# Three graph attention layers: the list of sources from five gathers of long pieces, and big and small blocks of nodes by turns

## The chip, the cores and the metric

The kernel runs on one core of a Trainium2 chip. The metric is the device time of one execution in microseconds, and the median of the runs is what counts. The engines are called as in the profile: PE is TensorE, DVE is VectorE, ACT is ScalarE, POOL is GpSimd and SP is SyncE. POOL issues all indirect DMAs (gathers), SP most of the plain ones.

## The reference

There are N = 6,250 nodes with 256 features each, and E = 100,000 edges given as `src` and `dst`, sorted by `dst`. A node has 16 incoming edges on average. Two layers with 4 heads of 64 features come first, with a self-loop added to each node, and an elu between them; then a residual and a layer norm; then a layer with 8 heads of 32 features, a residual and a layer norm:

```python
def _gatv2_layer(x, src, dst, n, Wl, Wr, att, b):          # layers 1 and 2
    xl = (x @ Wl).reshape(n, H, C)
    xr = (x @ Wr).reshape(n, H, C)
    e = jax.nn.leaky_relu(xl[src] + xr[dst], NEG_SLOPE)
    logits = jnp.einsum('ehc,hc->eh', e, att)
    # softmax of the logits over the edges of each dst -> alpha
    msg = xl[src] * alpha[:, :, None]
    return segment_sum(msg, dst).reshape(n, H * C) + b

def third_layer(h, W, a, src, dst):                         # layer 3
    Wh = jnp.einsum('nf,hfd->hnd', h, W)
    e = jax.nn.leaky_relu(s1[:, src] + s2[:, dst], ALPHA)   # s1 = Wh.a1, s2 = Wh.a2
    # softmax over the edges of each dst -> attn
    return segment_sum(attn[:, :, None] * Wh[:, src], dst)

x = _layernorm(x + layer2(elu(layer1(x))))
x = _layernorm(x + third_layer(x))
```

All is float32. The indices are known only on the chip.

## The kernel before, in words

**Columns and blocks.** The nodes are sorted by their number of incoming edges and cut into 49 blocks of 128, one node to a partition. `columns` works out from E and N alone how many sources per node a block may have to hold: 27 for the first block (its few longer lists are treated apart, with one extra gathered row), then 25, 24, 23, 22, 21, 21, and so on down to 9 in the last. The sum is 803. A block of c columns needs c gathers: each brings one row of the layer's table (1 KB and a little more) for each of 128 nodes.

**The plan** (`make_plan`). It finds each node's sources and its place in the sorted order. The steps that matter here run in this order on DVE: `count` (incoming edges of each node, from products on PE), `begin_i` (L993, where a node's list begins), then the sort: `oh`, `cum` (scans), `place_f`, `to`, then three wide products `to_hi`, `given`, `to_lo` (L1080), which PE multiplies into `pp` (L1085): the node that stands at each sorted place. Then come `lacking` and `fill` for six spans of nine blocks (L1013: entries beyond a node's count are set to "no node"), `node_i` from `pp`, and `fits`, a check on which the main path rests. Beside this POOL gathers the lists: 49 times (L998) a piece of CM = 38 sources for each of 128 nodes, where the program's own numbering puts node b*128 + p on partition p. `fill` writes each span to `near_d` in HBM.

```python
    for k in range(NB):                                    # L998
        nc.gpsimd.indirect_dma_start(out=near[:, k, :], in_=listed, in_offset=begin_i[:, k])
```

(The call is shortened.) `tables(n)` puts the next n of the 49 blocks of the first table x @ Wl through PE (transposes and a product), ACT (copies) and SP (writes to `xl_d`). The order of every engine is the order of the program text; no scheduler reorders it. 27 tables stand ahead of the sort's last products, 22 behind `pp`. Spans 0 and 1 of `fill` stand before `node_i`, span 2 after the `fits` products, span 3 seven tables later, spans 4 and 5 behind the last table.

**The layers** (`tile_by_degree`). Each of layers 1 and 2 goes through the 49 blocks in order. POOL gathers one block ahead of the one in work, as far as a ring of 9 row tiles (`rows`, 9 columns to a tile) has room:

```python
            for b in range(NB):
                if b + 3 < NB: start(b + 3)
                if b + 1 < NB: gather(b + 1)               # POOL, L1235
                if b + 2 == NB: follow()                   # early gathers of the next layer
                if b + 1 < NB: ready(b + 1)                # the next block's own products
                rows, cut, wt, new = attend(b)             # DVE: z, lg; ACT: exps
                if b: rest = end(b - 1, acc, den)
                den = new(); nc.vector.reciprocal(den, den)
                acc = weighted_sum(...)                    # DVE: g * wt; PE: acc, L1418
```

For each row tile `attend` makes three passes on DVE (L1504 to L1506): a maximum that does the leaky ReLU, a product with `att`, and a sum to the logits `lg`. ACT makes the exps into `wt`. `weighted_sum` multiplies rows by weights on DVE (L1411) and ACT (L1410), and PE adds the columns up into `acc` with one product of the identity per column. The last steps of block b-1 (its row of the next layer's table, over PE, ACT and SP) run beside this. A gather of a layer reads any row of that layer's table, so it has to wait until all 49 blocks have been written by the layer before.

`EARLY = (14, 12, 11)` softens that: in layer 1, `sort_sources` sorts the lists of blocks 0, 1 and 2 by number, and the first 14, 12 and 11 columns of these, which lie in all blocks but the last four (`LATE`), are gathered at the end of the layer before (the index tile is `soon`). That is 37 early gathers for layer 2 and 37 for layer 3.

Layer 3 has no z passes, its logits come with the gathered row. DVE multiplies rows by weights (L1433) and adds columns up (L1442). POOL puts each finished block out, one put to a block.

Of the kernel before, what the change touches and what calls it, by code (L numbers as in the profile page):

```python
# [26 lines left out]
F32 = mybir.dt.float32  # L27
BF16 = mybir.dt.bfloat16
I32 = mybir.dt.int32
# [6 lines left out]
P = 128  # L36
# [4 lines left out]
RUNS = 64  # L41
EARLY = (14, 12, 11)
LATE = 4


def columns(E, N, NB):

    mean = E / N
    pmf = [math.exp(-mean)]
    for k in range(1, 200):
        pmf.append(pmf[-1] * mean / k)
    over, sd = [], []
    for c in range(199):
        p = sum(pmf[c + 1 :])
        g = sum((k - mean) * pmf[k] for k in range(c + 1, 200))
        over.append(N * p)  # L60
        sd.append(math.sqrt(max(N * (p * (1.0 - p) - g * g / mean), 0.0)))
    cols = []
    for b in range(NB):
        most = P * b
        cols.append(next(
            c for c in range(199) if (over[c] + 3.5 * sd[c] <= most if b else over[c] < 0.01)
        ))
    low = max((c for c in range(199) if N - over[c] <= P // 4), default=0)
    high = next(c for c in range(199) if over[c] <= P // 4)
    pmf += [0.0] * 200  # L70
    held = next(
        c for c in range(199)
        if N * sum((k - c) * pmf[k] for k in range(c, 200))
        + 3.5 * math.sqrt(N * sum((k - c) ** 2 * pmf[k] for k in range(c, 200))) <= P
    )
    assert cols[1] <= held < cols[0]
    return cols, low, high, held

# [636 lines left out]
def make_plan(  # L715
# [20 lines left out]
    assert (NP + 1) << SHIFT < 1 << 24 and NB % PART == 0  # L736

    one = ctx.enter_context(tc.tile_pool(name="plan_one", bufs=1))
    tmp = ctx.enter_context(tc.tile_pool(name="weights", bufs=2))
# [5 lines left out]
    dram = ctx.enter_context(tc.tile_pool(name="list_dram", bufs=1, space=DRAM))  # L745
    list_d = dram.tile([-(-E // CM) * CM + CM], I32, name="list_d")

# [123 lines left out]
    if rest:  # L871
# [8 lines left out]
    diff = iota("diff_f", [P, P], [[1, P]], mult=-1)  # L880
    nothing = filled_tile("nothing", [1, list_d.shape[0] - E], 0, I32)
    nc.gpsimd.memset(next_e, NP)
    left(0, nc.gpsimd)
    a = next(d for d in range(512, 0, -16) if E % d == 0)
    nc.scalar.dma_start(list_d[E:].unsqueeze(0), nothing)
    nc.scalar.dma_start(
        list_d[:E].rearrange("(a b) -> a b", a=a), src.rearrange("(a b) -> a b", a=a)
    )
    each = iota("each", [P, P, T], [[1, P], [0, T]], dtype=BF16)
    x_end = filled_tile("x_end", [P, F], 0.0)  # L890
    far = filled_tile("far", [P, CM], NP, I32)
    ranks = iota("ranks", [P, CM], [[1, CM]])
    ones = filled_tile("ones_f", [P, P], 1.0)
    ones_b = filled_tile("ones_b", [P, P], 1.0, BF16)
# [47 lines left out]
    for what in "lar":  # L942
# [3 lines left out]
    part = one.tile([P, 3, RUNS], I32, name="part")  # L946
    nc.vector.tensor_scalar(
        part[:, 0, :], run_i, SHIFT, P - 1, op0=OP.logical_shift_right, op1=OP.bitwise_and
    )
    nc.vector.tensor_single_scalar(part[:, 1, :], run_i, SHIFT + 7, op=OP.logical_shift_right)  # L950
    nc.vector.tensor_single_scalar(part[:, 2, :], run_i, (1 << SHIFT) - 1, op=OP.bitwise_and)
# [25 lines left out]


    pc = ps.tile([P, 2, NB], F32, name="pc", tag="ph")
    nc.tensor.matmul(pc[:, 0, :], ones, count, start=True, stop=True)  # L980
    nc.tensor.matmul(pc[:, 1, :], above, count, start=True, stop=True)
    key = one.tile([P, NB], BF16, name="key_b")
    nc.vector.tensor_scalar(key, count, float(high), float(low), op0=OP.min, op1=OP.max)
    nc.vector.tensor_scalar(key, key, -1.0, float(high), op0=OP.mult, op1=OP.add)
    block = one.tile([P, NB], F32, name="block")
    nc.vector.tensor_copy(block, pc[:, 0, :])
    upto = one.tile([P, NB], F32, name="upto")
    nc.vector.tensor_tensor_scan(upto, ones_k[:, :NB], block, 0.0, op0=OP.mult, op1=OP.add)
    from_f = one.tile([P, NB], F32, name="from_f")
    nc.vector.tensor_sub(from_f, upto, block)  # L990
    nc.vector.tensor_add(from_f, from_f, pc[:, 1, :])
    begin_i = one.tile([P, NB], I32, name="begin_i")
    nc.vector.tensor_scalar(begin_i, from_f, float(E), 0.0, op0=OP.min, op1=OP.max)  # L993
    near = one.tile([P, NB, CM], I32, name="near")
    no = one.tile([P, NB, CM], I32, name="no")
    listed = list_d.rearrange("(a b) -> a b", b=CM)
    for k in range(NB):
        nc.gpsimd.indirect_dma_start(  # L998
            out=near[:, k, :], out_offset=None, in_=listed,
            in_offset=bass.IndirectOffsetOnAxis(ap=begin_i[:, k : k + 1], axis=1),  # L1000
        )
    spans = [(k, min(NB, k + 9)) for k in range(0, NB, 9)]
# [8 lines left out]
    def fill(k0, k1):  # L1011
        shape = [P, k1 - k0, CM]
        nc.vector.copy_predicated(  # L1013
            near[:, k0:k1, :], no[:, k0:k1, :], far[:, None, :].to_broadcast(shape)
        )
        nc.sync.dma_start(
            near_d[k0 * P : k1 * P, :CM].rearrange("(k p) c -> p k c", p=P).bitcast(I32),
            near[:, k0:k1, :],
        )


    tables(1)
    oh = one.tile([P, KEYS, NB], BF16, name="oh")
    nc.vector.tensor_tensor(
        oh, steps, key[:, None, :].to_broadcast([P, KEYS, NB]), op=OP.is_equal
    )
    ohf = oh.rearrange("p k b -> p (k b)")
# [22 lines left out]
    nc.vector.tensor_single_scalar(piece[:, 0, :], place, P - 1, op=OP.bitwise_and)  # L1050
    nc.vector.tensor_single_scalar(piece[:, 1, :], place, 7, op=OP.logical_shift_right)
    nc.vector.tensor_scalar(vals[:, 2, :], count, 255.0, None, op0=OP.min)
    to = one.tile([P, 2, NB], BF16, name="to")
# [3 lines left out]
    with nc.allow_non_contiguous_dma(reason="one number to a row"):  # L1057
        nc.scalar.dma_start(
            xl1_d[:NP, W2:].rearrange("(b p) w -> p b w", p=P), place_f.unsqueeze(2)
        )  # L1060
# [25 lines left out]
    for k in spans:  # L1086
        lacking(*k)
    fill(*spans[0])
    fill(*spans[1])
    got = one.tile([P, 3, NB], F32, name="got")  # L1090
    nc.vector.tensor_copy(got, pp)
    nc.vector.scalar_tensor_tensor(
        node_i, got[:, 1, :], float(P), got[:, 0, :], op0=OP.mult, op1=OP.add
    )

    wrong = one.tile([P, KE + NB + 1], F32, name="wrong")
    nc.vector.tensor_tensor(wrong[:, : KE - 1], dst_e[:, : KE - 1], dst_e[:, 1:], op=OP.is_gt)
    nc.vector.tensor_tensor(wrong[:, KE - 1 : KE], dst_e[:, KE - 1 :], next_e, op=OP.is_gt)  # L1100
    nc.vector.tensor_tensor(wrong[:, KE : KE + NB], got[:, 2, :], most, op=OP.is_gt)
    nc.vector.tensor_scalar(
        wrong[:, KE + NB :], upto[:, NB - 1 :], float(E), None, op0=OP.not_equal
    )
# [14 lines left out]
    right(1)  # L1119
    fill(*spans[2])  # L1120
    for c in range(2):
# [4 lines left out]
    tables(7)  # L1126
    fill(*spans[3])
    for k, b in enumerate(biases):
# [8 lines left out]
    tables(NB)  # L1137
    for k in spans[4:]:
        fill(*k)


@with_exitstack
def tile_by_degree(
# [52 lines left out]
    few_row = consts.tile([P, max(W2 + 1, A1)], F32, name="few_row")  # L1196
    soon = consts.tile([P, len(EARLY), max(EARLY)], I32, name="soon")
    late = consts.tile([P, len(EARLY)], F32, name="late")
# [118 lines left out]
    def begin(own, table, width):  # L1317

        for b, n in enumerate(EARLY):
            begun[b] = row_tiles(b, own)  # L1320
            gather_rows(b, *begun[b], own, table[:AHEAD], soon, width, 0, n)

    def sort_sources(work, ps, b):
# [9 lines left out]
        for r in range(0, CK, 8):  # L1333
# [5 lines left out]
        nc.vector.tensor_single_scalar(spots[:, b, :n], places[:, :n], KEY, op=OP.logical_shift_right)  # L1339
        e = EARLY[b]  # L1340
        nc.vector.tensor_single_scalar(soon[:, b, :e], spots[:, b, :e], AHEAD - 1, op=OP.min)
        nc.vector.tensor_single_scalar(
            late[:, b : b + 1], spots[:, b, e - 1 : e], float(AHEAD), op=OP.is_ge
        )
        if b + 1 == len(EARLY):
            pb = ps.tile([P, b + 1], F32, name="pb", tag="tp")
            nc.tensor.matmul(pb, ones, late, start=True, stop=True)
            bad = work.tile([P, 1], F32, name="bad")
            nc.vector.reduce_sum(bad, pb, axis=AX.X)
            nc.vector.tensor_single_scalar(done, bad, 0.0, op=OP.is_equal)  # L1350
# [115 lines left out]
    def layer2(i, table, of, width, start, own, finish, follow):  # L1466
# [5 lines left out]
        with ExitStack() as es:  # L1472
# [24 lines left out]
            def attend(b):  # L1497
# [29 lines left out]
                if i == 0:  # L1527
                    for g, (s0, s1) in zip(rows, cut):
                        s = max(s0, 1)
                        nc.scalar.copy(spots[:, b, s - 1 : s1 - 1], g[:, s - s0 : s1 - s0, W2])  # L1530
                    if 0 < b <= len(EARLY):
                        sort_sources(work, pst, b - 1)
# [260 lines left out]
```

## Time and profile before

| | before |
|---|---|
| median of 3 runs | 3365.79 us (3364.47 to 3366.1) |
| profiled execution | 3880.55 us, span 3878.7 us |
| mean granted TensorE clock in it | 0.665 |
| busy in the span | PE 1481.8, DVE 2836.2, ACT 1091.1, POOL 2530.5 us |
| first row gather of layer 1 | 154.5 us from the span's start |
| layer 1, first to last reciprocal | 201.8 to 1494.1 us |
| layer 2 | 1542.0 to 2704.1 us |
| layer 3 | 2747.5 to 3862.5 us |

The rows from the third on come from the one profiled execution, which took 515 us more than the median. The times within it are therefore for comparing parts with each other, and not shares of the 3365.79 us. A line of a group reads: source line, engine, operation, output<-input, count, then busy time in all, mean duration in ns, and the idle time of the engine just before these instructions, with what ended most of it. A line of a timeline reads: start, duration, engine, source line, operation, and in brackets the idle time before it and what ended it.

### The profile page before, as it was taken

What the parts mean: (1) busy time and instruction counts of PE and PEld (TensorE: products, weight loads), DVE (VectorE), ACT (ScalarE), POOL (GpSimd) and SP (SyncE); (2) the same over time, 40 slices, a digit from 0 to 9 for tenths busy, and PEclk for the clock granted to TensorE, in tenths of its full rate; (3) what the DMA queues carried; (4) which work ended last, traced back from release to release, by engine and by line L of the source; (5) the groups of instructions that cost most, each with busy time, mean ns of one, the idle gap of its engine ahead of it and who ended that gap; (6) DMA issues with size and microseconds to landing.
All of it is one profiled execution on the core that took longest, in us unless ns stands there. A gap on an engine that the chain in (4) does not pass through costs nothing.

```text
span 3878.7 us, 23608 instructions
## 1 busy us (share of the span) xinstructions
PE 1481.8 (38%) x5130; PEld 1113.8 (29%) x5130; DVE 2836.2 (73%) x2648; ACT 1091.1 (28%) x4176; POOL 2530.5 (65%) x2613
## 2 busy tenths in 40 slices
PE   6324665556667763355544545554000000000000
PEld 5213444434555542343433433443000000000000
DVE  6228988668888876899876988896676565666665
ACT  3113444334445442243433434443000000000000
POOL 6464666666666645666666666664777777777774
PEclk8656877778788886676666677776555555555555
DMA  8532333333434334333433434442343333333332
GB/s 188 109 92 78 98 104 104 100 99 103 105 102 108 104 79 109 100 106 104 112 107 105 111 107 110 109 111 74 101 108 101 96 97 96 97 97 96 97 97 57
DMA packets 196123, 395.60 MB, mean 102 GB/s; under 512 B 63036, under 2 KB 115514, under 8 KB 195956
## 3 DMA queue, kind: packets, MB, share of 16 engines
q0 software_dynamic: 122048, 338.04, 33.2%
q1 hardware_dynamic: 66226, 54.22, 5.1%
q10 hardware_dynamic: 7698, 1.74, 0.4%
q8 instruction: 45, 0.74, 0.1%
q14 instruction: 106, 0.87, 0.1%
HBM read 353.82 MB, written 40.42 MB: 102 GB/s over the span
## 4 chain that ended last, share of the span: by engine, by line
issue 20%; POOL 20%; DVE 13%; PE 10%; another core or an unknown queue 6%; ACT 5%; DMA 1%; DVEq 0%; POOLq 0%; ACTq 0%
POOL g L1235 18%; PE acc L1418 6%; DVE z L1505 4%; DVE z L1504 4%; DVE lg L1506 3%; PE pm L1362 3%; ACT g L1410 2%; ACT wt L1381 2%; DVE g L1411 1%; POOL out L1733 1%; DMA g<-xl_d,near_r 1%; DVE weighted L1433 1%; ACT xT L1357 0%; PE pt L1355 0%
## 5 line engine op out<-in xcount | busy, mean ns | idle before, releaser
L1235 POOL DMA_INDIRECT g<-xl_d,near_r x1569 | 1487.4, 948 | 858.7 <-issue 454.3
L1418 PE MATMUL acc<-g,ident 128*128 128x256 f32 x3408 | 1015.9, 461 | 765.3 <-issue 282.7
L1418 PEld LDWEIGHTS acc<-g,ident 128*128 128x128 f32 x3408 | 774.4, 234 | 1004.2 <-issue 522.3
L1235 POOL DMA_INDIRECT g<-whs_d,near_r x766 | 793.2, 1036 | 284.2 <-issue 250.0
L1410 ACT ACTIVATE g<-g,by 128x64 f32<-128x64 f32 x2056 | 545.1, 337 | 316.1 <-issue 310.8
L1504 DVE TENSOR_TENSOR z<-g,pr 128x1820 f32<-128x1820 f32 (+4 forms) x234 | 497.1, 2125 | 19.1 <-DMA g<-xl_d,near_r 10.0
L1505 DVE TENSOR_TENSOR z<-z,at 128x1820 f32<-128x1820 f32 (+4 forms) x234 | 497.4, 2126 | 8.0
L1506 DVE TENSOR_REDUCE lg<-z 128x28 f32<-128x1820 f32 (+4 forms) x234 | 497.3, 2125 | 8.1
L1442 DVE TENSOR_REDUCE acc_v<-weighted 128x256 f32<-128x4096 f32 (+15 forms) x49 | 343.7, 7014 | 16.5 <-remote 8.3
L1411 DVE TENSOR_TENSOR g<-g,wt 128x1792 f32<-128x1792 f32 (+8 forms) x234 | 348.4, 1505 | 2.9
L1391 ACT ACTIVATE wt<-lg 128x128 f32<-128x128 f32 (+17 forms) x49 | 14.0, 285 | 851.0 <-DVE top L1374 391.5
L1703 DVE TENSOR_TENSOR lg<-g,s_r 128x56 f32<-128x56 f32 (+4 forms) x111 | 22.1, 213 | 315.1 <-DMA g<-whs_d,near_r 272.5
L1357 ACT COPY xT<-pt 128x256 f32<-128x256 f32 x147 | 54.9, 374 | 688.5 <-remote 342.2
L1433 DVE TENSOR_TENSOR weighted<-g,wt 128x1792 f32<-128x1792 f32 (+4 forms) x111 | 226.6, 2056 | 0.1
L1571 DVE RECIPROCAL den<-den 128x4 f32<-128x4 f32 x98 | 17.4, 177 | 212.9 <-ACT wt L1381 165.2
L1381 ACT ACTIVATE wt<-lg,top 128x19 f32<-128x19 f32 (+14 forms) x392 | 116.0, 296 | 190.8 <-DVE lg L1506 74.3
L1362 PE MATMUL pm<-wcat,xT 128*128 128x260 f32 x392 | 136.0, 505 | 56.3 <-ACT xT L1357 49.8
L1362 PE MATMUL pm<-wh_cat,xT 128*128 128x272 f32 x196 | 77.5, 531 | 183.8 <-ACT xT L1357 95.5
L1537 DVE TENSOR_TENSOR h<-acc,den 128x256 f32<-128x256 f32 x98 | 40.7, 416 | 126.2 <-remote 112.8
L1362 PEld LDWEIGHTS pm<-wcat,xT 128*128 128x128 f32 x392 | 94.8, 255 | 90.5 <-ACT xT L1357 64.6
L1362 PEld LDWEIGHTS pm<-wh_cat,xT 128*128 128x128 f32 x196 | 42.8, 242 | 203.0 <-ACT xT L1357 104.7
L1362 PE MATMUL pl<-wcat,xT 128*128 128x260 f32 x196 | 64.0, 455 | 55.5 <-issue 40.4
(232 smaller groups left out, 1548.4 us busy)
## 6 DMA issues: line engine op xcount, KB each, us to landing
g<-xl_d,near_r POOLq DMA_INDIRECT x1569
g<-whs_d,near_r POOLq DMA_INDIRECT x766
whs_d<-row SPq DMA_DIRECT2D x49, 132.0 KB
xl_d<-xl SPq DMA_DIRECT2D x49, 130.0 KB
xl_d<-row SPq DMA_DIRECT2D x49, 130.0 KB
xr_d<-row SPq DMA_DIRECT2D x49, 130.0 KB
two<-xl_d SPq DMA_DIRECT2D x49, 130.0 KB
two<-xr_d SPq DMA_DIRECT2D x49, 130.0 KB
```

What stands on the lines that cost most here:

```text
L1235: nc.gpsimd.indirect_dma_start(out=g[:, j + own - s0, :width], out_offset=None, in_=table, in_offset=source(of, b, j),)
L1357: nc.scalar.copy(xT, pt)
L1362: nc.tensor.matmul(pm, xT[:, c, :], w[:, c, :], start=c == 0, stop=c == 1)
L1381: nc.scalar.activation(wt[:, :, h], lg[:, :S, h], AF.Exp, bias=top[:, h : h + 1], accum_out=den[:, h : h + 1],)
L1410: nc.scalar.mul(g4[:, t, h, :], g4[:, t, h, :], by[:, t - m, h : h + 1])
L1411: nc.vector.tensor_mul(g4[:, :m], g4[:, :m], wt[:, s0 : s0 + m, :].unsqueeze(3).to_broadcast([P, m, H, F // H]),)
L1418: nc.tensor.matmul(acc, ident, g4[:, t], start=s0 + t == 0, stop=s0 + t == S - 1 and not more)
L1433: nc.vector.tensor_mul(prod[:, s0 - base : s1 - base, :].rearrange("p t (h d) -> p t h d", h=H), g[:, :n, :F].rearrange("p t (h d) -> p t ...
L1442: nc.vector.reduce_sum(part, prod[:, : s1 - base, :].rearrange("p s f -> p f s"), axis=AX.X)
L1504: nc.vector.tensor_max(z, g[:, :n, :W2], xr[:, None, :].to_broadcast([P, n, W2]))
L1505: nc.vector.tensor_mul(z, z, at[:, None, :].to_broadcast([P, n, W2]))
L1506: nc.vector.reduce_sum(lg[:, s0:s1, :], z.rearrange("p t (h d) -> p t h d", h=H2), axis=AX.X)
```

## The change

It has three parts.

1. **Five gathers instead of 49.** The nodes are numbered p*49 + b during the plan, so that partition p holds 49 nodes in sequence and their lists lie one after the other in the sorted edge list. Five gathers (one for each ten nodes) bring pieces of LONG = 309 sources. Node k of a piece would begin at 16k (less a lead of 64) if each node had 16 edges; the real place differs by 0 to 127, `off_i`. DVE moves each list into place bit by bit: for the bit of 64, while it copies out of the piece (10 copies and 10 predicated copies), then for the bits of 32 to 1 with six predicated copies over all 50 slots. All this stands before the sort (`cum` and so on) in DVE's order; `oh` is moved ahead too.
2. **Big and small blocks by turns.** `columns` returns 27, 9, 25, 10, 24, 10, 23, 11, 22, 11, 21, 12, ... 16, 16 in place of the descending order, in all three layers and their tables. In the plan `place_f` and `piece` are changed to match (four small DVE instructions).
3. **EARLY** becomes {0: 14, 2: 12}: block 1 now has 9 columns and none early; two blocks are sorted in layer 1 instead of three.

All six fills now stand together ahead of `node_i`, and so, in SP's queue, between the 27th and the 28th table. The diff, cut to its core:

```diff
-EARLY = (14, 12, 11)
+EARLY = {0: 14, 2: 12}
@@ columns
-    return cols, low, high, held
+    turns = [0] * NB
+    for r, c in enumerate(cols):
+        turns[min(2 * r, 2 * NB - 1 - 2 * r)] = c
+    return turns, low, high, held
@@ make_plan
+    SEGS, STEP, BITS = 5, 10, 7
+    LEAD = 1 << BITS - 1
+    MEAN = E // N
+    LONG = MEAN * (STEP - 1) + CM + 2 * LEAD - 1
+    WIDE = CM + LEAD - 1
...
-    nc.tensor.matmul(pc[:, 0, :], ones, count, start=True, stop=True)
-    nc.tensor.matmul(pc[:, 1, :], above, count, start=True, stop=True)
+    total = one.tile([P, 1], F32, name="total")
+    nc.vector.reduce_sum(total, count, axis=AX.X)
+    nc.tensor.matmul(pc[:, 1:], above, total, start=True, stop=True)
+    nc.tensor.matmul(pc[:, :1], ones, total, start=True, stop=True)
...
+    for k in range(SEGS):
+        nc.gpsimd.indirect_dma_start(
+            out=piece_of[:, k, :], out_offset=None, in_=listed,
+            in_offset=bass.IndirectOffsetOnAxis(ap=begin_i[:, k : k + 1], axis=1),
+        )
...
+    nc.vector.tensor_scalar(off_i, off, 0.0, float(2 * LEAD - 1), op0=OP.max, op1=OP.min)
+    for k in range(BITS):
+        nc.vector.tensor_scalar(
+            bit[:, k], off_i, k, 1, op0=OP.logical_shift_right, op1=OP.bitwise_and
+        )
+    moved = one.tile([P, SEGS, STEP, WIDE], I32, name="moved")
+    for k in range(STEP):
+        for first_at in (0, LEAD):
+            data = piece_of[:, :, MEAN * k + first_at : MEAN * k + first_at + WIDE]
+            if first_at == 0:
+                nc.vector.tensor_copy(moved[:, :, k, :], data)
+            else:
+                nc.vector.copy_predicated(
+                    moved[:, :, k, :],
+                    bit[:, BITS - 1, :, k : k + 1].to_broadcast([P, SEGS, WIDE]), data,
+                )
+    every = moved.rearrange("p s j w -> p (s j) w")
+    bits = bit.rearrange("p b s j -> p b (s j)")
+    for k in range(BITS - 2, -1, -1):
+        n = CM + (1 << k) - 1
+        nc.vector.copy_predicated(
+            every[:, :, :n], bits[:, k, :].unsqueeze(2).to_broadcast([P, SEGS * STEP, n]),
+            every[:, :, 1 << k : (1 << k) + n],
+        )
+    near = every[:, :NB, :CM]
-    for k in range(NB):
-        nc.gpsimd.indirect_dma_start(
-            out=near[:, k, :], out_offset=None, in_=listed,
-            in_offset=bass.IndirectOffsetOnAxis(ap=begin_i[:, k : k + 1], axis=1),
-        )
...
-            near_d[k0 * P : k1 * P, :CM].rearrange("(k p) c -> p k c", p=P).bitcast(I32),
+            near_d.rearrange("(p k) c -> p k c", k=NB)[:, k0:k1, :CM].bitcast(I32),
...
+    nc.vector.tensor_scalar(back, piece[:, 1, :], -2.0, float(2 * NB - 1), op0=OP.mult, op1=OP.add)
+    nc.vector.tensor_single_scalar(piece[:, 1, :], piece[:, 1, :], 2.0, op=OP.mult)
+    nc.vector.tensor_tensor(piece[:, 1, :], piece[:, 1, :], back, op=OP.min)
...
-    fill(*spans[0])
-    fill(*spans[1])
+    for k in spans:
+        fill(*k)
...
-    fill(*spans[2])
...
-    fill(*spans[3])
...
-    for k in spans[4:]:
-        fill(*k)
@@ tile_by_degree
-        for b, n in enumerate(EARLY):
+        for b, n in EARLY.items():
             begun[b] = row_tiles(b, own)
             gather_rows(b, *begun[b], own, table[:AHEAD], soon, width, 0, n)
...
-                    if 0 < b <= len(EARLY):
+                    if b - 1 in EARLY:
                         sort_sources(work, pst, b - 1)
```

## The prediction

> **What bounds the kernel now.** I read the page's groups first, then busy time by stage (first to last reciprocal of each layer), then the timeline where stages meet.
>
> ```profile
> L1235 POOL DMA_INDIRECT g<-xl_d,near_r x1569 | 1487.4, 948 | 858.7 <-issue 454.3
> L1235 POOL DMA_INDIRECT g<-whs_d,near_r x766 | 793.2, 1036 | 284.2 <-issue 250.0
> L1418 PE MATMUL acc<-g,ident 128*128 128x256 f32 x3408 | 1015.9, 461 | 765.3 <-issue 282.7
> L1504 DVE TENSOR_TENSOR z<-g,pr 128x1820 f32<-128x1820 f32 (+4 forms) x234 | 497.1, 2125 | 19.1 <-DMA g<-xl_d,near_r 10.0
> ```
>
> The columns after the bar are busy us, mean ns of one, idle us ahead of it and its releaser. The z work (L1504) hardly waits; the gathers wait for rows mostly in layers 1 and 2.
>
> ```profile
> core 0: us, PE busy (x) PEld busy (x) DVE busy (x) ACT busy (x) POOL busy (x), PEclk, DMA share, GB/s
> 201.80:1494.10 1292.30, 775.59 (x2630) 573.48 (x2630) 992.75 (x892) 511.05 (x1955) 803.04 (x847) 0.77 0.38 99
> 1542.00:2704.10 1162.10, 585.65 (x1970) 448.86 (x1970) 977.14 (x792) 456.49 (x1839) 739.34 (x781) 0.70 0.39 106
> 2747.50:3862.50 1115.00, 1.95 (x4) 1.00 (x4) 718.40 (x754) 65.50 (x191) 824.23 (x796) 0.50 0.36 96
> ```
>
> Layers 1 and 2 hold nearly 1,000 us of VectorE (DVE) work each, layer 3 only 718. A gather takes 0.95 us and the next starts 0.30 later, so 803 gathers, 49 output puts and one extra row ask 853 × 1.25 = 1,066 us of POOL in layer 3: **VectorE sets layers 1 and 2, POOL layer 3**.
>
> ```profile
> 103.71 0.54 DVE L1013 COPY_PREDICATED near<-no,far 128x342 int32<-128x342 int32 x1 [8.19 <-DMA near<-list_d,begin_i]
> 115.88 0.33 DVE L1013 COPY_PREDICATED near<-no,far 128x152 int32<-128x152 int32 x1 [4.16 <-DMA near<-list_d,begin_i]
> 149.98 0.24 POOL L1182 IOTA numbers<- 128x128 f32 x1 [35.72 <-DMA near_d<-near]
> 2692.40 0.95 POOL L1235 DMA_INDIRECT g<-whs_d,soon  x1 [0.30 <-issue]
> 2722.39 0.94 POOL L1235 DMA_INDIRECT g<-whs_d,near_r  x1 [29.04 <-DMA whs_d<-row]
> ```
>
> Before layer 1, the fills (L1013) wait for the 49 list gathers. At layer 3's border POOL finishes the early gathers at 2693 and then idles 29 us: those gathers are free.
>
> The profiled execution took 3880.55 us (span 3878.7), 515 more than the median 3365.79. Its timeline has stretches (91 to 119, for one) in which PE, ACT, DVE and SP step along 0.7 or 1.4 us apart with nothing to wait for. I take this to be the profile's own cost, so I price from undisturbed stretches and add the sum to the median. An undisturbed chain is: start of the row gathers about 126, layer 1's first block 45, its other blocks 1,035, two borders near 20 each, layer 2 1,060, layer 3 816 × 1.25 = 1,020, drain 12: 3,340, near the median.
>
> **What the skill says.** "SBUF — State Buffer", section "Who interferes with whom": a VectorE instruction with two SBUF inputs contends with a GpSimd instruction that reads SBUF. The trace agrees: the list gathers, otherwise 0.94 us, took 2.27 to 6.29 beside the plan's wide bf16 products (L1080, 6.68 us, among them). "DMA: Bandwidth & Descriptors", section "Specifications", wants at least 512 B per transfer for line rate. A list piece is 38 int32, 152 B, now, and 309, 1,236 B, afterwards. The trace shows 6 to 9 us from gather to landing in the busy plan, 2.6 when DMA was idle; it has no such long piece.
>
> **The change, part by part.**
>
> *Plan.* 44 of 49 list gathers go: 44 × 1.25 = 55 us of POOL. Five remain, issued at about 40 to 46 and landed by 49 to 52. The bits and `oh` fill that wait. Then DVE moves the pieces: 10 copies and 10 predicated copies of 5×101 elements, 6 predicated copies of 50 × (69, 53, 45, 41, 39, 38) = 14,250. L1013 gives 342 elements in 0.54 us and 152 in 0.33, so 0.16 fixed plus 0.88 elements per ns: 16 to 17 us for the six, 0.73 for one of 505; a plain copy I put at 0.55 to 0.6. Sum: 7.3 + 6 + 17 = **30 us**, none hidden, since DVE is in order and everything up to `to_lo` stands behind it. Formerly that chain began at 41 while the gathers ran. It is 11.2 us (scans, place), 17.2 (to_hi, given, to_lo), then 6 (lacking, fills) and right/left. So `to_lo` ends near 108 instead of 69.6, DVE's plan near 120.
>
> PE's order does not change: `pp` and 22 of the 49 input tables are queued behind `to_lo`. At 1.1 us a table, plus `pp` 4.9 and other products, the last table is written near 143 and landed near 146. Before, undisturbed, the start waited for the last list gather (114), the fill (116.2) and landings to about 122, then three reads of `near_d` to 126. The six fills now stand in SP's queue between the 27th and 28th table, ready before the latter. **Plan: +20**, between −10 (if the 149.98 of the trace is also the true start) and +28.
>
> *Turns, layers 1 and 2.* The number of columns, row tiles and instructions is the same. DVE's 1,012 and 994 us over 48 blocks are near POOL's 853 × 1.25 = 1,066 and 804 × 1.25 = 1,005; but they are close block by block too (25 columns: 28.4 DVE, 31 POOL; 10: 14.6 and 12.5), so mixing big and small gains only what the ring of 9 row tiles could not already smooth: **−8** for both (0 to −30).
>
> Against it stands the loop behind a big block; its durations come from undisturbed blocks of the timeline. After block b's reciprocal its PE sum (L1418) starts 2.3 us later and takes 0.53 us a column; the next block's products queue behind it on PE, then the ACT copies (xT, the row) and the exps take 4.2 + 1.9. For 26 columns (own row included) that is 2.3 + 13.8 + 6.1 = 22.2 us. DVE meanwhile has 5.4 us to the end of b's weighting, then the next block's z and 2.1. With an equal neighbour z is 22 to 24, so nothing waits. With 11 columns z is 10.1, and DVE waits 22.2 - 17.6 = 4.6. Worked out so for the pairs (26, 11), (25, 11), (24, 12), (23, 12), twice (22, 13), (21, 13) and twice (21, 14), with z of 10.1 to 12.4: 4.6, 4.3, 3.0, 2.6, 1.4, 1.4, 0.9, 0.2, 0.2, together 18 in layer 1. In layer 2 the own products are absent and 4.2 becomes 3.0: 3.4, 3.2, 1.9, 1.7, 0.5, 0.5, together 11. The following big block has more z than the loop needs, so nothing returns. **+29** (0 to +45, depending on PE's granted clock).
>
> *Ends of layers.* The last block has 16 neighbours instead of 9, so PE's last sum and the weighting ahead of the next table's last rows are 7 columns longer, some 4.5 us at each of two borders: **+9**. In layer 3 the drain after the last gather grows with 16 columns of weighting and reduction (10 us for nine): **+5**.
>
> *EARLY 37 to 26.* The 11 gathers dropped ran in POOL's 29 us of idle time; they return in layer 3, where POOL is the bound: 11 × 1.25 = **+13.75**. At layer 2's border DVE has block 0 ahead of them: 0. One sort less (301.1 to 304.1): −2.
>
> Sum: 20 − 8 + 29 + 9 + 5 + 14 − 2 = **+67**, so 3365.8 + 67 = 3,433.
>
> **Rivals.** *Faster.* The start does gain and blocks by turns smooth more than I allow. For it: POOL stands 858.7 us idle before row gathers, more than one block's difference explains, and a big block is POOL-bound, a small one DVE-bound. If the trace's start is true (−10), balance gives 22 in layer 1 and 10 to 25 in layer 2, and PE's clock hides the loop, then with the +28 of ends and early gathers kept, −15 to −30: 3,336 to 3,351. It decides from a stall per small block below 1 us. Against it: z waits only 19.1 us over the whole run. *No change.* Gains of balance equal the 28 us of the ends and the start is even: 3,366. *Slower, but without the loop through PE* (a higher granted clock than the trace's 0.77 and 0.70): plan, ends and early gathers alone: 20 + 28 − 8 = +40, 3,406. *The plan does not do what it says*: were the shift beyond 7 bits for some node, the fall-back path would run as well, many times slower. The shift sums the counts of at most nine nodes of 16 sources each; with a spread near 4 per node that is 12, and the 64 that it may reach is five times as much, so I give this nothing.
>
> **How the numbers follow.** Full sum 0.40 (3,433); slower without the loop 0.25 (3,406); about no change 0.05; faster 0.30 (3,343). A measurement tells 0.2% here, 6.7 us. Range 3,340 to 3,470: the faster case's middle up to the sum with the loop's upper bound and the plan's.
>
> **What would show each step.** Right: last list landing by 52, `to_lo` ending 105 to 112, row gathers starting near 145; DVE waiting 1 to 5 us for exps (ACT) in each small block that follows one of over 20 columns; 26 gathers from `soon` per border and a longer POOL wait after them; layer 3's row gathers back to back at 1.25. Wrong: a start before 130, layers 1 and 2 shorter than before, or no wait on ACT in small blocks.

## The result and the profile after

The change makes the kernel slower: 3448.73 us (median of 5 runs, 3445.57 to 3450.3) against 3366.1 us for the kernel before on the same chip (5 runs, 3364.47 to 3370.33). The ratio is 1.0242, with a 95% interval of 1.0227 to 1.0257: 82.6 us more, where 67 had been forecast.

The profile of before shown ahead of the prediction, and the first and third group of experiments below, come from executions in which every kernel, the kernel before included, takes some 500 us longer (3,870 and 3,887 us instead of 3,366), so the time of each run is compared with the kernel before of its own group, and the stages of the changed kernel are laid beside profiles of the second and fourth group.

The groups on the page of the changed kernel (columns as before; L1305 is the gather, L1488 PE's sum, L1574 the first z pass):

```profile
L1305 POOL DMA_INDIRECT g<-xl_d,near_r x1580 | 1496.6, 947 | 552.0 <-issue 435.9
L1488 PE MATMUL acc<-g,ident 128*128 128x256 f32 x3408 | 957.6, 451 | 818.7 <-DVE sd L1531 467.8
L1305 POOL DMA_INDIRECT g<-whs_d,near_r x777 | 738.9, 951 | 271.4 <-issue 226.6
L1574 DVE TENSOR_TENSOR z<-g,pr 128x1820 f32<-128x1820 f32 (+4 forms) x234 | 497.2, 2125 | 15.8 <-DMA g<-xl_d,near_r 8.0
```

The work is the same as before: the same 234 z passes of 2,125 ns, the same 3,408 products. There are 11 gathers more from `near_r` for each of `xl_d` and `whs_d` (1,580 for 1,569, 777 for 766): those that are no longer early. What changed is waiting. Busy time by stage of the changed kernel, first to last reciprocal of each layer:

```profile
211.20:1273.50 1062.30, 674.43 (x2616) 540.10 (x2616) 988.74 (x876) 475.28 (x1946) 794.95 (x838) 0.83 0.45 120
1324.10:2356.10 1032.00, 541.72 (x1956) 432.85 (x1956) 975.32 (x792) 445.32 (x1832) 738.75 (x781) 0.75 0.45 119
2403.00:3418.90 1015.90, 1.95 (x4) 1.00 (x4) 714.19 (x753) 65.58 (x191) 768.75 (x807) 0.50 0.40 107
```

And the same view of plan_moves_late_again (an experiment below: blocks in descending order and 37 early gathers, as in the kernel before):

```profile
179.10:1232.00 1052.90, 685.75 (x2630) 548.14 (x2630) 992.14 (x893) 478.12 (x1956) 793.75 (x837) 0.83 0.45 120
1279.60:2302.50 1022.90, 549.17 (x1970) 438.28 (x1970) 976.50 (x792) 447.61 (x1839) 724.85 (x766) 0.74 0.43 118
2346.50:3348.90 1002.40, 1.95 (x4) 1.00 (x4) 718.71 (x754) 65.51 (x191) 757.88 (x796) 0.50 0.39 107
```

Layer 1 is 9.4 us longer, layer 2 9.1 and layer 3 13.5, though DVE's busy time (third busy column) is a little lower in each. The two borders, read as the gaps between the windows, are 50.6 for 47.6 and 46.9 for 44.0. The plan has no part in this: turns_again (below), with blocks by turns and the plan of 49 list gathers, has layers of 1,061.7, 1,031.4 and 1,017.3 us.

Most of the rest lies ahead of layer 1. The timeline of the changed kernel there (start, duration, instruction, idle time before and what ended it):

```profile
45.37 0.95 POOL L1019 DMA_INDIRECT piece_of<-list_d,begin_i  x1 [0.30 <-issue]
...
50.76 0.48 DVE L1048 COPY moved<-piece_of 128x505 int32<-128x505 int32 x1 [8.36 <-DMA piece_of<-list_d,begin_i]
...
62.13 17.90 DVE L1058 COPY_PREDICATED moved<-bit,moved 128x3450 int32<-128x3450 int32 x6
...
81.18 0.20 PE L1091 MATMUL pk<-oh,ones_b 128*128 128x54 bf16 x1 [38.87 <-DVE cum L1092]
...
109.33 6.09 PE L1152 MATMUL pp<-given,to_lo 128*128 128x147 bf16 x49 [9.74 <-DVE to_lo L1147]
...
136.45 0.38 ACT L862 COPY xl<-pm 128x260 f32<-128x260 f32 x1 [6.41 <-DMA xl_d<-xl]
...
159.20 0.97 POOL L1665 DMA_INDIRECT near_r<-near_d,node_i  x1 [9.79 <-DMA xl_d<-xl]
...
163.95 0.94 POOL L1305 DMA_INDIRECT g<-xl_d,near_r  x1 [1.29 <-DVE few_n L1316]
```

DVE waits 8.4 us for the pieces, moves for 29, and only then scans. PE, whose third `pk` needs DVE's scan, stands 38.9 us with its tables queued behind. It makes up for this: all 27 tables ahead of `pp` are done when it waits 9.7 us more for `to_lo`. Behind `pp` stand the other 22 tables; ACT waits there up to 6.4 us for old rows to be written out. POOL reads its indices when the last `xl_d` row lands, at 159.2, and gathers rows from 163.95.

### The profile page after: what moved, and what is told of

Its sections match the earlier page's. It is cut to its first block, busy times and chain, and to the rows that moved or that the text cites. A ratio compares the mean times of both kernels' runs of the same rounds, so it can differ in the third digit from the quotient of the medians.

```text
span 3446.7 us, 23586 instructions
## 1 busy us (share of the span) xinstructions
PE 1336.2 (39%) x5130; PEld 1067.4 (31%) x5130; DVE 2866.2 (83%) x2677; ACT 1043.4 (30%) x4160; POOL 2411.4 (70%) x2597
## 4 chain that ended last, share of the span: by engine, by line
POOL 29%; DVE 25%; issue 19%; PE 10%; DMA 7%; ACT 3%; DVEq 0%; POOLq 0%; ACTq 0%
POOL g L1305 28%; PE acc L1488 9%; DVE z L1574 7%; DVE z L1575 6%; DVE lg L1576 6%; DMA g<-xl_d,near_r 4%; ACT wt L1451 2%; DVE weighted L1503 2%; DMA g<-whs_d,near_r 2%; DVE g L1481 1%; POOL out L1803 1%; DVE top L1444 1%; PE pm L1432 1%; DVE acc_v L1512 0%; DMA near_r<-near_d,node_i 0%
## 5 line engine op out<-in xcount | busy, mean ns | idle before, releaser
L1305 POOL DMA_INDIRECT g<-xl_d,near_r x1580 | 1496.6, 947 | 552.0 <-issue 435.9
L1488 PE MATMUL acc<-g,ident 128*128 128x256 f32 x3408 | 957.6, 451 | 818.7 <-DVE sd L1531 467.8
L1488 PEld LDWEIGHTS acc<-g,ident 128*128 128x128 f32 x3408 | 780.4, 232 | 996.7 <-issue 499.4
L1305 POOL DMA_INDIRECT g<-whs_d,near_r x777 | 738.9, 951 | 271.4 <-issue 226.6
L1574 DVE TENSOR_TENSOR z<-g,pr 128x1820 f32<-128x1820 f32 (+4 forms) x234 | 497.2, 2125 | 15.8 <-DMA g<-xl_d,near_r 8.0
L1576 DVE TENSOR_REDUCE lg<-z 128x28 f32<-128x1820 f32 (+4 forms) x234 | 497.3, 2125 | 8.1
L1480 ACT ACTIVATE g<-g,by 128x64 f32<-128x64 f32 x2040 | 496.2, 334 | 0.0
L1451 ACT ACTIVATE wt<-lg,top 128x18 f32<-128x18 f32 (+14 forms) x392 | 115.5, 295 | 505.2 <-DVE top L1444 487.4
L1461 ACT ACTIVATE wt<-lg 128x112 f32<-128x112 f32 (+17 forms) x49 | 14.0, 285 | 816.3 <-DVE lg L1460 816.3
L1432 PE MATMUL pm<-wcat,xT 128*128 128x260 f32 x392 | 99.0, 396 | 22.6 <-ACT xT L1427 22.6
L1432 PEld LDWEIGHTS pm<-wcat,xT 128*128 128x128 f32 x392 | 70.5, 189 | 42.8 <-ACT xT L1427 34.2
L1451 ACT ACTIVATION_READ_ACCUMULATOR wt<-lg,top 128x1 f32 x392 | 73.4, 187 | 0.0
L1803 POOL DMA_INDIRECT out<-y,node_i x49 | 49.8, 1017 | 30.2 <-ACT y L1534 16.1
```

The lines of the kernel that those rows point to most:

```text
L1305: nc.gpsimd.indirect_dma_start(out=g[:, j + own - s0, :width], out_offset=None, in_=table, in_offset=source(of, b, j),)
L1432: nc.tensor.matmul(pm, xT[:, c, :], w[:, c, :], start=c == 0, stop=c == 1)
L1451: nc.scalar.activation(wt[:, :, h], lg[:, :S, h], AF.Exp, bias=top[:, h : h + 1], accum_out=den[:, h : h + 1],)
L1480: nc.scalar.mul(g4[:, t, h, :], g4[:, t, h, :], by[:, t - m, h : h + 1])
L1488: nc.tensor.matmul(acc, ident, g4[:, t], start=s0 + t == 0, stop=s0 + t == S - 1 and not more)
L1574: nc.vector.tensor_max(z, g[:, :n, :W2], xr[:, None, :].to_broadcast([P, n, W2]))
```

## The experiments

**First group: the parts one by one, and the kernel before again** (the kernel before took 3869.96 us, median of 36 runs).

*before_look*, no edit.

> The kernel before, unchanged, for a second profile of it. If the steps of 0.7 and 1.4 us in its first profile were the profile's own, this one spans about 3365 us, starts its row gathers near 126, and shows layers 1, 2 and 3 some 1,035, 1,060 and 1,015 long. If they are the kernel's, it spans 3,880 again.

It took 3865.45 us, spanned 3863.6 and started its row gathers at 153.2; the 36 timed runs take as long (3,848 to 3,884). So the steps of 0.7 and 1.4 us are not the profile's own cost, as the prediction had taken them to be. They do not belong to the kernel either, which took 3,366 us in the comparison with the changed one.

*plan_only*

```diff
-EARLY = {0: 14, 2: 12}
+EARLY = {0: 14, 1: 12, 2: 11}
-    return turns, low, high, held        # columns
+    return cols, low, high, held
-    back = ...                           # and the three steps after it
```

> Only the plan is changed (five gathers, moves on VectorE, fills together); blocks in descending order and 37 early gathers as before. Theory A (the change loses about 35 us ahead of layer 1 and 45 in the layers): first row gather at 160 to 164 instead of about 126, time 3,400. Theory B (the plan costs what was forecast, 20, and the layers lose over 60): 3,386.

3878.82 us, ratio 1.0027 (1.0013 to 1.0041): 5 to 16 us more, less than either theory said. First row gather at 170.1, 17 later than in before_look. Starts scatter here, though: with one and the same plan of 49 gathers they lie between 146.3 (turns_only) and 159.7 (turns_half_sum) in the profiles of the first and third group.

*turns_only*

```diff
 # the kernel before, with only this of the change: EARLY = {0: 14, 2: 12}, return turns,
 # and back/min ahead of "to"; the 49 list gathers stay
```

> Only the order of blocks is changed, with the 26 early gathers that go with it; the plan with 49 gathers as before. Theory A: 3,366 + 45 = 3,411. Theory B: 3,366 + 62 = 3,428. If mixing big and small blocks gained in itself and the plan had eaten it: below 3,366.

3932.53 us, ratio 1.0187 (1.0134 to 1.0241), 52 to 93 us more: theory B's 62 rather than A's 45, though turns_again, below, comes nearer to A. Blocks by turns lose by themselves; nothing was gained that the plan ate.

*early_two*

```diff
-EARLY = (14, 12, 11)
+EARLY = (14, 12)
```

> The kernel before with EARLY = (14, 12): 26 early gathers, nothing else changed. Theory: the 11 gathers come back in layer 3 at 1.25 us each, one sort of 3 us goes: 3,366 + 14 - 3 = 3,377. Rival: POOL has 11 gathers' room somewhere in layer 3, and the time stays within 3 us of 3,366 or falls by the sort.

3886.08 us, ratio 1.0048 (1.0032 to 1.0064), or 12 to 25 us: in accord with the 11 at its low end, and the rival of no cost falls. How much more than 11 it is stays unsettled.

**Second group** (the kernel before took 3369.93 us).

*turns_again*: turns_only once more.

> Only the order of blocks with its 26 early gathers, once more, as the base for the next. Theory (the 82 us of the whole change split into about 35 for the plan and 45 for the layers): where the kernel before takes 3,366, this takes 3,411. Rival (the layers lose over 60, the plan 20 or less, as in the call before): 3,430 or more.

3409.22 us, ratio 1.0115 (1.0098 to 1.0132), 39 us: the theory's 3,411, not the rival's 3,430. What is left for the plan is 82.6 - 39 = 43. Its start, with the 49 list gathers, stands for that of the kernel before (before_ends_late, which has blocks in descending order, starts its row gathers at 133.8):

```profile
129.58 0.24 POOL L1194 IOTA numbers<- 128x128 f32 x1 [15.02 <-DMA near_d<-near]
...
134.13 0.95 POOL L1247 DMA_INDIRECT g<-xl_d,near_r  x1 [0.31 <-issue]
```

The row gathers begin at 134.1, and 163.95 in the changed kernel: 29.8 us later.

*turns_ends_late* and *before_ends_late*, the same edit in two kernels:

```diff
-                if b + 1 < NB:
-                    ready(b + 1)
                 rows, cut, wt, new = attend(b)
+                if b + 1 < NB:
+                    ready(b + 1)
+                    later.pop()()
+                if ends:
+                    ends.pop()()
...
-                if last:
-                    last[0]()
+                if last and b + 1 < NB:
+                    ends.append(last[0])
```

> Blocks by turns, with ACT's order changed: the next block's own products (ready) and the last steps of block b-1 are issued after the exps of the block in work instead of ahead of them, so that the exps no longer wait behind copies that wait for PE's sum of the block before. Theory (loop behind a big block): 15 to 29 us less than turns_again. Rival (the small blocks wait for rows or for DVE): within 5 us of turns_again, or longer.

> The same edit of ACT's order in the kernel before, as a control. Theory: neighbours have equal z there, nothing waits in the loop, so within 7 us of the kernel before. Rival (the edit helps every block, by whatever it takes off ACT or PE): the same gain as between turns_ends_late and turns_again.

3821.46 and 3796.54 us, ratios 1.1339 (1.132 to 1.1358) and 1.1265 (1.1246 to 1.1283): the theory holds in neither kernel; turns_ends_late is longer, as its rival allowed, but for a reason that neither named. DVE's waits in layer 1 of before_ends_late (line that waited, releaser, us in all, times, longest):

```profile
DVE h L1623 <- ACT pos L1618: 324.0, 47, 8.0
DVE den L1575 <- ACT wt L1381: 30.6, 44, 0.7
```

The copies that I moved behind the exps now stand ahead of ACT's elu steps (`pos`), which DVE needs in the middle of the weighting, 7 us in each block; in layer 2 DVE waits 84.5 us for ACT's `sd`. The edit made a new wait larger than the one it was to remove, so it tells nothing of the loop. I had followed DVE's and PE's queues past the moved copies, and not ACT's own.

*plan_tables_ahead*

```diff
-    tables(12)
+    nc.sync.dma_start(x_end[: rows(NB - 1)], x[(NB - 1) * P :, :])
+    tables(NB)                            # no tables(...) after this; from plan_only
```

> Blocks in descending order, the plan with five gathers as in plan_only, but all 49 tables stand ahead of pp on PE and all fills behind them in SP's queue. Theory (the plan loses because 22 tables queue behind the moves on PE, and then behind the fills in SP's and the DMA queues): first row gather at 128 to 136 instead of about 160, within 10 us of the kernel before. Rival (VectorE's 30 us of moves are the loss wherever the tables stand): 25 us or more above the kernel before.

3406.89 us, ratio 1.011 (1.0093 to 1.0127), first row gather at 166.7: the theory as written fails, and the number is the rival's. Behind `pk` the tables still wait for the moves, and now `pp` waits for the tables:

```profile
110.96 2.57 DVE L1072 COPY_PREDICATED moved<-no,far 128x342 int32<-128x342 int32 x6
132.79 0.31 DVE L1146 COPY got<-pp 128x147 f32<-128x147 f32 x1 [19.26 <-PE pp L1140]
```

The fills, ready at 113.5, leave SP from 140.3 on, behind the tables' writes.

**Third group** (the kernel before took 3886.59 us).

*plan_tables_first* puts `tables(NB)` ahead of the first `pk` in PE's order; the small loads of SP stand ahead of it, the fills are last.

> Descending order, five gathers, moves ahead of the sort as in the changed kernel, but all 49 tables stand ahead of the sort's first product pk on PE, so that none waits for the moves; fills last on SP. Theory (PE stood idle from 42 to 81 us at pk, behind the moves, and 14 tables with it): PE's tables end near 85, fills at 114, first row gather at 132 to 138, 3,372 to 3,380. Rival (PE's stall is hidden and SP's or DMA's backlog sets the start): first row gather at 155 or later, 3,400.

3866.89 us, ratio 0.995 (0.9931 to 0.997), first row gather at 143.8: 26 us earlier than plan_only in the first group, more than the scatter of starts. The moves stand where they stood, so their 30 us alone do not make the late start; it needs tables queued behind them. Whether the tables' place on PE or the fills' on SP did it, this run alone does not separate; the fills stood last in plan_tables_ahead too, and that started late.

*plan_moves_late* keeps PE's `pk`, then all tables, then `pp`, and moves the moves:

```diff
     for b in range(NB):
         nc.tensor.matmul(pp, to_lo[:, b, :], given[:, b], ...)
+    moved = one.tile([P, SEGS, STEP, WIDE], I32, name="moved")
+    ...                                   # the 26 moving instructions, from before "tables(1)"
```

> Descending order, five gathers, but the moves stand behind the sort and its products (after to_lo) in VectorE's order, the tables run between pk and pp without waiting for the moves, and the fills are SP's last writes. Theory (the five gathers lose only because the sort, and PE's tables with it, stand behind the moves): DVE's fills end near 105 instead of 114, first row gather at 120 to 128 instead of 164 (134 with 49 gathers), so 6 to 14 us less at the start; 5 us more at POOL's last drain, as in the other kernels with five gathers; 3,356 to 3,367 where the kernel before takes 3,370. Rival (30 us of moves are a loss wherever they stand): 3,390 or more.

3862.88 us, ratio 0.9936 (0.9919 to 0.9953), first row gather at 135.8. Both kernels are faster than the kernel before of this group, so their rivals fall here; for the second the fourth group decides.

*turns_half_sum*, blocks by turns, leaves every second column out of PE's sum:

```diff
             for t in range(n):
+                if (s0 + t) % 2 and s0 + t != S - 1:
+                    continue
                 nc.tensor.matmul(acc, ident, g4[:, t], ...)
```

> Blocks by turns with the old plan; PE leaves out every second column of its sum in layers 1 and 2 (except the first and last), so the result lacks these columns; DVE, ACT and POOL do all they did. Theory (small blocks wait for exps behind the PE sum of the big block): the waits of up to 3.8 and 2.7 us ahead of the reciprocals of blocks 5 to 17 fall to the 0.7 and 0.4 of the other blocks, 18 us less, and the last sums at the two borders are some 4 us shorter each: 3,380 to 3,390 against 3,409. Rival (they wait for the copies or the row products, not for the sum): the waits stay, 3,400.

The time went the other way, 4022.18 us, ratio 1.0354 (1.0333 to 1.0375), against 1.0187 of turns_only: new pauses of up to 15 us stand ahead of big blocks there, whose cause is not settled, so the time can't be used. The waits that it was made for can be. Timeline lines of the reciprocals of blocks 5, 7 and 9 of layer 1, first in turns_only, then in turns_half_sum:

```profile
384.50 0.18 DVE L1583 RECIPROCAL den<-den 128x4 f32<-128x4 f32 x1 [4.80 <-issue]
442.18 0.18 DVE L1583 RECIPROCAL den<-den 128x4 f32<-128x4 f32 x1 [4.13 <-ACT wt L1393]
499.66 0.18 DVE L1583 RECIPROCAL den<-den 128x4 f32<-128x4 f32 x1 [3.31 <-issue]
```

```profile
394.61 0.18 DVE L1585 RECIPROCAL den<-den 128x4 f32<-128x4 f32 x1 [0.66 <-issue]
453.57 0.18 DVE L1585 RECIPROCAL den<-den 128x4 f32<-128x4 f32 x1 [0.67 <-issue]
505.40 0.18 DVE L1585 RECIPROCAL den<-den 128x4 f32<-128x4 f32 x1 [0.67 <-ACT wt L1393]
```

With half of PE's sum gone the three waits fall from 4.8, 4.1 and 3.3 us to 0.7. Ahead of blocks 4 and 8 there is no new pause (0.8 and 0.7 us), so blocks 5 and 9 did not get their time from one. For some of these lines the trace names no releaser; in turns_again the same three waits, 3.8, 3.3 and 1.9, all end with ACT's exps. PE's sum of the big block is what the small block waits for.

**Fourth group** (the kernel before took 3365.63 us): *plan_moves_late_again*.

> plan_moves_late once more, since in its first call every kernel was over 500 us longer than in the comparison of before and after. There it was 0.64% faster than the kernel before, and its first row gather came at 135.8 us against 153.2. Theory (most of that gain is in the start itself): where the kernel before takes 3,366 to 3,370, first row gather at 120 to 128 instead of 134, 3,356 to 3,367. Rival (the gain came from the pauses of that call, which a shorter plan meets less often): within 5 us of the kernel before, or slower by the 5 us of POOL's last drain.

3372.93 us, ratio 1.0022 (1.0012 to 1.0031). The start is a little earlier:

```profile
127.36 0.24 POOL L1237 IOTA numbers<- 128x128 f32 x1 [80.81 <-DMA near_d<-moved]
...
131.85 0.95 POOL L1290 DMA_INDIRECT g<-xl_d,near_r  x1 [0.30 <-DVE few_lack L1299]
```

That is 2.3 us before the 134.1 with 49 gathers, not 6 to 14. The fills are ready near 105, but SP issues the first at 104.1, then waits 8.3 us for a DMA semaphore (the trace puts its release down to the landing of `place_f`, which ACT had issued at 98.1 behind its tables), and the other five leave between 112.8 and 118.4 and land by 127. An earlier place for that DMA was not tried. The 5.1 us at POOL's last drain take the gain back and 2.8 more; of the 7.3 us by which it is slower, 4.5 stay open. So the rival's second form holds: no version run here beats a kernel before of 3,366 to 3,370 us. But the same five gathers and moves start the row gathers 32 us earlier than in the changed kernel (131.85 for 163.95): the loss at the start is one of order.

## Why the prediction was right, point by point

The direction, the mechanisms and the sum of turns held, the last by luck; the plan was sized too small.

| Term | forecast | measured | from |
|---|---|---|---|
| plan, start of layer 1 | +20 | +29.7 | first reciprocal 211.2, 181.5 in turns_again |
| plan, end of the program | not seen | +5.1 | POOL's last drain 6.35, 1.28 |
| turns, layers 1 and 2 | -8 + 29 - 2 | +9.4 + 9.1 | windows above |
| borders | +9 | +3.0 + 2.9 | windows above |
| layer 3, early gathers | +14 | +13.5 | windows above |
| drain of layer 3 | +5 | +5.5 | 27.8 against 22.3 after the last reciprocal |
| sum | +67 | +78 | 82.6 by the medians |

Each column of the layers is from one execution, and repeated executions of one kernel here lie 3 to 5 us apart; the 4 us between 78 and 82.6 are left open. They may be the 4.5 us left open in plan_moves_late_again, since the table takes its layers from there: 1.2 of those lie after the last reciprocal, where it takes 22.3 us, and before_ends_late 16.0 with a drain 5.1 us shorter.

**The plan.** Up to `to_lo` the steps came as told: lists landed by 50.8 (by 52 forecast), the moves took 29 (30), `to_lo` ended at 109.3 (108), 37.7 us later than in turns_again. PE's 38.87 us at `pk` had not been seen, but cost nothing that shows: PE stands ready 9.7 us before `to_lo`, as it does with 49 gathers. What was sized too small is the stretch behind `to_lo`, "the last table is written near 143 and landed near 146". PE's `pp` in turns_again, and SP's last writes of tables there and in the changed kernel:

```profile
71.66 4.82 PE L1097 MATMUL pp<-given,to_lo 128*128 128x147 bf16 x49 [10.00 <-DVE to_lo L1092]
116.97 4.16 SPq L849 DMA_DIRECT2D xl_d<-xl  x6
```

```profile
154.13 4.10 SPq L863 DMA_DIRECT2D xl_d<-xl  x6
```

From the end of `to_lo` to the end of the last write are 49.0 us in the changed kernel (109.3 to 158.2) and 49.5 in turns_again (71.6 to 121.1). The prediction took 35, from 1.1 us for a table; it left out that ACT waits there for old rows to be written, 12.2 us in the changed kernel and 10.9 in turns_again. The change did not lengthen this stretch, although all six fills, 6,272 pieces of 152 B, now stand ahead of its writes and only two did before. It moved it, by 37.7 us. About 8 of these come back: with 49 gathers the last two fills stand behind the stretch (SP issues them from 121.5), and POOL waits for their landing, until 129.6; with five, the fills are ahead, and POOL waits for the last table alone. So 29.8 us reach the first row gather. The three index reads that follow, 4.75 us, were not counted in the forecast either. In all the start was forecast near 146 and came at 163.95.

The forecast start of before, 126 instead of the trace's 154.5, was nearer to the 134.1 of turns_again than the trace, though the reason given for it (the profile's own cost) was wrong. Being 8 us too early, it hid 8 of the 18 us that the new start is late: as a difference the plan looks only 10 us off.

**The loop behind a big block.** Mechanism right, size too large: 18 and 11 forecast. DVE's waits for exps, layer 1 then layer 2, first in the changed kernel, then in plan_moves_late_again:

```profile
DVE den L1641 <- ACT wt L1451: 42.5, 47, 3.8
...
DVE den L1641 <- ACT wt L1451: 27.6, 48, 2.7
```

```profile
DVE den L1626 <- ACT wt L1436: 33.0, 46, 1.6
...
DVE den L1626 <- ACT wt L1436: 18.8, 48, 2.0
```

The difference is 9.5 and 8.8 us. Block by block the waits in layer 1 are 3.8, 3.3 and 1.9 in blocks 5, 7 and 9, where 4.3, 3.0 and 2.6 were forecast. But every block, in both kernels, waits 0.7 anyway, so only what exceeds this is new; the forecast had counted from zero. And block 3, with 4.6 forecast, does not wait at all: there DVE is busy sorting the lists of block 2 until after the exps are done. (The nine terms of the forecast add up to 18.6; without block 3, and less 0.7 for each of the other eight, they are 8.4.)

**Balance.** -8 was given for mixing; nothing of it is seen. DVE's account closes without it: in layers 1 and 2 it waits 9.5 and 8.8 us longer for exps and 3.9 and 1.4 in other places, and is busy 3.4 and 1.2 less, which makes 10.0 and 9.0 for the 9.4 and 9.1 measured. That 19 were forecast for both layers and 18.5 measured is luck: two errors cancelled. The borders were sized too large, at 4.5 us each for 3.0 and 2.9; no run separates why.

**Early gathers.** The time was right, but its premise has to be corrected: POOL's 29 us of idle time at the border stand only in the profile of 3,880 us. In plan_moves_late_again 37 early gathers fill POOL's time to the landing of the table almost exactly; in the changed kernel 26 leave a gap (timelines at layer 3's border, plan_moves_late_again first):

```profile
2321.38 0.94 POOL L1290 DMA_INDIRECT g<-whs_d,near_r  x1 [0.81 <-DMA whs_d<-row]
```

```profile
2377.82 0.94 POOL L1305 DMA_INDIRECT g<-whs_d,near_r  x1 [35.00 <-DMA whs_d<-row]
```

The gap is 34 us longer, of which the 11 gathers are 13.8. The rest probably comes from POOL's order of blocks at the end of the layer, which no run separates; it costs nothing, because POOL waits for the table anyway. That the 11 gathers come back in layer 3 is shown by early_two in direction; the 13.5 us are those of the windows.

**The rivals.** *Faster* needed a start at least even and less than 1 us of wait per small block; the start was 30 later and six waits are over 1 us in layer 1. *No change* falls with it. *Slower without the loop* (3,406) was too low: the loop does bite, although PE's granted clock in layers 1 and 2 is 0.83 and 0.75, above the 0.77 and 0.70 of the first trace. *The plan does not do what it says* would have been many times slower.

## What to carry to other kernels

When work is moved onto an engine in an in-order plan, follow what is queued behind the product that it delays, to the last landing, and take the length of that stretch from a trace and not from the price of one piece: here the 22 tables behind `pp` took 49 us where 35 had been summed, and it took as long with the old plan (49.5 us in turns_again). A long wait on an engine (PE's 38.9 us at `pk`) need not be the loss: the engine may have to wait later anyway. A shared resource freed (44 gathers, 55 us of POOL) is worth only what waited for it last; and the mix of big and small tiles gained nothing here, where each size was already balanced, while it exposed small ones to the tail of the big ones. Before pricing idle time from a profile, see that it takes as long as the timed runs; this one took 515 us more.

## What the runs showed of the hardware that was not expected

- POOL's last long DRAIN, at the end of the program, takes 1.28 us in all eight profiles with 49 short list gathers and 6.35 in all six with five long ones, whatever the order of blocks. The 5.1 us lie open at the end of the program. Why is not settled.
- A gather of 1,236 B pieces occupies POOL no longer than one of 152 B: 0.95 us, and 0.30 to the next. The five landed 4.4 us after the last was issued (46.3 to 50.8).
- The fills, 128 x 9 pieces of 152 B each (the last one 128 x 4), land slowly. In plan_moves_late_again two of the six landings can be read, 9.2 and 4.7 us after issue; POOL, which waits for the last of them, goes on at 127.4, 9 us after SP has issued it.
